# Four graph layers in one kernel: other due dates and buffer reserves for a list scheduler

## The chip, the cores and the metric

The kernel runs on one core of one Trainium2 chip. The metric is the device time of one execution in microseconds. Three executions of the kernel before took 2530.77, 2531.31 and 2533.68 us, so its median is 2531.31 us.

## What is computed

There are 128 graphs of 128 nodes with 256 features each, in fp32. Every layer normalizes its input, applies a ReLU and adds its result to the input:

```python
h = relu(layernorm(x)); x = x + L0(h, adj)   # 3 steps: m = h @ W[i]; a = A^T m; h = GRU(a, h)
h = relu(layernorm(x)); x = x + L1(h, adj)   # sum over relations r: (adj == r) @ h @ W1[r], + bias
h = relu(layernorm(x)); x = x + L2(h, adj)   # attention: softmax(mask(leaky(ei + ej))) @ (h W^T)
h = relu(layernorm(x)); x = x + L3(h, adj)   # the same attention with other weights
```

`GRU` has three gates of two 256x256 products each, so layer 0 holds most of the matrix work. In this text "layer 0" is the recurrent layer and "the attention" or "the later layers" are L1, L2 and L3.

## The kernel before, in words

Four graphs (`G = 4`) make a group of 512 columns; there are 32 groups, numbered 0 to 31. One group passes through loading, layer 0 (three steps, function `step`), the relation layer (`neighbours`, L666, products at L634 and L644) and two attention layers (`attention`, L979, and `attend`, L997), and is then stored (L1087). The gate products of layer 0 are written in a form with seven block products in place of eight; all their matmuls are issued at L825. L767 is the product with the adjacency, also of layer 0.

Nothing in this program runs in the order in which the code is written. `build` (L307) makes a list of operations, each with its engine (some may go to ScalarE or VectorE, as the planner chooses), an assumed duration, its dependences and the buffers that it uses. `Plan.order` (L137) then runs a list scheduler over them in Python, before anything is on the chip, and its result is the fixed order of the instructions on each engine. Four things decide that order:

- **Rank** (L143 to L148). An operation's "way" is the longest chain of assumed durations from it to the end of its own group. Its rank is `group * PERIOD` less its way, less a `rush` that is nonzero for a few operations. The lowest rank goes first. So `group * PERIOD` is a due date of the group, and groups are due 36000 ns apart. (Only differences of rank matter; a group is not finished every 36 us.)
- **Choice** (L225 to L256). On each engine the scheduler looks at the operations whose predecessors are placed. Those that can start within 100 ns of the engine's free time compete by rank; the others come after them by start time. At most `AHEAD = 5` groups are open at a time.
- **Buffers.** A buffer takes a slot of its pool when its first operation is placed and returns it after its last. Pools: 8 PSUM `banks`, 5 `xs`, 7 `adjs`, 29 `big` (128x512 fp32), 11 `wide` (128x1024), 10 `small`, 4 `masks`, 4 `lines`. `SPARE` gives, for the first five pools in that order, how many slots a group later than the oldest open one has to leave free (L236); with `DEEP = 1` the number doesn't grow with the distance.
- **Pieces** (L742, L975). A group is handled as a whole in the later layers, or in pairs of graphs, or singly. With `SINGLE = 2` and `SPLIT = 2`, groups 30 and 31 are handled singly and all others whole. Whole groups turn their attention matrices by a DMA transpose (L362 to L372) and spread a row of terms by two DMAs (L1019, L1021); pairs and singles do both on TensorE (L1012, L1069). The last step of layer 0 in a group that isn't handled whole is turned on TensorE as well (L954).

All four engines' orders, and the transfers issued by SyncE, come from the same plan. The first operations also hold a scan of the whole adjacency (L539 to L548, the last four with a `rush` of 90000), which finds whether all values are 0 or 1. At that point the program branches: `plan.order` is run once for the usual inputs and once, with the operations before the branch as a given `prefix`, for general ones. The inputs here take the usual branch. Some operations (`plan.shared = False`) are planned only after it.

Of the kernel before, what the change touches and what calls it, by code (L numbers as in the profile page):

```python
# [35 lines left out]


OWN = {"PE": 0, "ACT": 125, "DVE": 125, "POOL": 80, "SP": 2500, "ACTQ": 2500}
PERIOD = 36000
AHEAD = 5  # L40
SINGLE = 2
SPLIT = 2
LINE, SPREAD = 0, -1000
TURN = -2000
RUSH = 90000
EARLY = 0
SPARE = (0, 0, 0, 2, 0)
DEEP = 1
LOAD = 2000
BRANCH = 3000  # L50
# [2 lines left out]
def seen(o, h):  # L53
    return o.late + (LAG[o.eng] + HOP[h.eng] if h.engs != (o.eng,) else OWN[o.eng])
# [43 lines left out]
class Plan:  # L98
# [6 lines left out]
    def op(self, eng, ns, fn, r=(), w=(), after=(), port=None, rush=0, late=0):  # L105

        o = Op(*((eng, ns) if isinstance(eng, tuple) else ((eng,), (ns,))), fn, self.group)  # L110
        o.port = eng == "POOL" if port is None else port
        o.rush, o.late = rush, late
        if self.shared:
            o.key = self.keys
            self.keys += 1
        deps = set(after)
        for items, writes in ((r, False), (w, True)):
            for item in items:
                buf, parts = item if isinstance(item, tuple) else (item, None)
                for other, wrote, theirs in buf.uses:  # L120
                    if buf.alone and o.engs + other.engs != ("PE", "PE"):
                        deps.add(other)
                    elif (writes or wrote) and other is not o:
                        if parts is None or theirs is None or parts & theirs:
                            deps.add(other)
                buf.uses.append((o, writes, parts))
                if buf not in o.bufs:
                    o.bufs.append(buf)
                    buf.left += 1
        o.deps = sorted(deps, key=lambda d: d.wait)  # L130
        o.wait = len(self.ops)
        for d in deps:
            d.heirs.append(o)
        self.ops.append(o)
        return o

    def order(self, pools, cut=None, prefix=()):  # L137

        for o in reversed(self.ops):  # L143
            way = max((h.rank + seen(o, h) for h in o.heirs if h.group == o.group), default=0)
            o.rank = way + o.ns
        for o in self.ops:
            o.rank = o.group * PERIOD - o.rank - o.rush
            o.wait = len(o.deps)  # L148
        free = {id(p): [0.0] * len(p) for p in pools}
        spare = {id(p): n for p, n in zip(pools, SPARE)}  # L150
        left = {}
        for o in self.ops:
            left[o.group] = left.get(o.group, 0) + 1
        at = dict.fromkeys(LAG, 0.0)
        port = 0.0
        open_ = {e: [] for e in LAG}
        held = {}
        for o in self.ops:
            if not o.wait:
                held.setdefault(o.group, []).append(o)  # L160
        first = 0

        def admit(o):
            if o.group < first + AHEAD:
                for e in o.engs:
                    open_[e].append(o)
            else:
                held.setdefault(o.group, []).append(o)

        for g in range(AHEAD):  # L170
            for o in held.pop(g, []):
                admit(o)
        done = []

        def place(o, eng, end):
            nonlocal first, port
            for e in o.engs:
                open_[e].remove(o)
            o.eng = eng
            o.end = at[eng] = end  # L180
            if o.port and eng != "ACT":
                port = max(port, end)
            for b in o.bufs:
                b.left -= 1
                if not b.left and id(b.pool) in free:
                    last = max(u.end + u.late + LAG[u.eng] + 60 for u, _, _ in b.uses)
                    free[id(b.pool)][b.slot] = last
            for h in o.heirs:
                h.ready = max(h.ready, o.end + seen(o, h))
                h.wait -= 1  # L190
                if not h.wait:
                    admit(h)
            left[o.group] -= 1
            done.append(o)
            while first in left and not left[first]:
                first += 1
                for x in held.pop(first + AHEAD - 1, []):
                    admit(x)

        def take(b, slot):  # L200
            b.slot = slot
            free[id(b.pool)][slot] = float("inf")

        shared = {o.key: o for o in self.ops if o.key is not None}
        for theirs in prefix:
            o = shared[theirs.key]
            for b, other in zip(o.bufs, theirs.bufs):
                if b.slot is None:
                    take(b, other.slot)
            place(o, theirs.eng, theirs.end)  # L210
            for b, other in zip(o.bufs, theirs.bufs):
                assert b.left or not other.left, "given away too early"
        before = len(done)

        def branch():
            now = max(at[e] for e in ("PE", "ACT", "DVE", "POOL"))
            for e in at:
                at[e] = max(at[e], now + BRANCH)
            return len(done)

        ahead = AHEAD
        if prefix:
            branch()
            ahead = 1
        while len(done) < len(self.ops):  # L225
            best = None
            for eng, cands in open_.items():
                pick = None
                for o in cands:
                    if cut and o.key is None or o.group >= first + ahead:  # L230
                        continue
                    r = o.ready
                    for b in o.bufs:
                        if b.slot is None:

                            kept = spare.get(id(b.pool), 0) * min(o.group - first, DEEP)  # L236
                            r = max(r, sorted(free[id(b.pool)])[kept])
                    if r == float("inf"):
                        continue
                    start = max(at[eng], r, port if o.port and eng != "ACT" else 0)  # L240
                    key = (start if start > at[eng] + 100 else 0, o.rank)
                    if pick is None or key < pick[0]:
                        pick = (key, start, o)
                if pick and (best is None or pick[1] < best[0]):
                    best = (pick[1], pick[2], eng)
            if cut and cut.end and (best is None or best[0] > cut.end + LOAD):
                cut = None
                before = branch()
                continue
            assert best is not None, "no operation can start"  # L250
            start, o, eng = best
            for b in o.bufs:
                if b.slot is None:
                    slots = free[id(b.pool)]
                    take(b, min(range(len(slots)), key=slots.__getitem__))
            place(o, eng, start + o.times[o.engs.index(eng)])  # L256
        return done, before
# [3 lines left out]
def kernel(  # L261
# [45 lines left out]
    def build(general):  # L307
# [227 lines left out]
        for f in range(F):  # L535
# [6 lines left out]
        op("DVE", 120, lambda: nc.vector.tensor_reduce(  # L542
            top.t[:, 0:1], most.t, AX.X, ALU.max), r=[most], w=[top], rush=RUSH)
        op("PE", 109, lambda: nc.tensor.transpose(pm.t[0:1, 0:P], top.t[:, 0:1], ident.t),
           r=[top, ident], w=[pm], rush=RUSH)
        op("DVE", 200, lambda: nc.vector.tensor_reduce(
            top.t[0:1, 1:2], pm.t[0:1, 0:P], AX.X, ALU.max), r=[pm], w=[top], rush=RUSH)
        verdict = op("DVE", 80, lambda: nc.vector.tensor_scalar(  # L548
            found, top.t[0:1, 1:2], 1.0, None, ALU.is_gt), r=[top], rush=RUSH)

# [185 lines left out]
        def group(gi):  # L736
# [4 lines left out]
            xt, ai, aiT = state.pop(gi)  # L741
            pieces = singly if gi >= NG - SINGLE else pairs if gi >= NG - SPLIT else whole  # L742

# [230 lines left out]
            late = [o for o, _, _ in hT.uses[:1]]  # L974
            duos = singly if gi >= NG - SINGLE else pairs  # L975
            (relations if general else neighbours)(gi, xt, ai, aiT, m0, m3, late, pieces, duos)
# [175 lines left out]
```

## Time and profile before

| what | value |
|---|---|
| median of three executions | 2531.31 us |
| the profiled execution: its own time | 2530.32 us |
| the profiled execution: span from first to last instruction | 2528.5 us |
| TensorE busy, share of the span | 2481.2 us, 98% |
| VectorE busy | 2280.3 us, 90% |
| ScalarE busy | 1815.1 us, 72% |
| GpSimd busy | 490.6 us, 19% |
| mean granted TensorE clock | 0.993 |
| last matmul of layer 0 (group 31, L825) starts | 2471.36 us |
| last residual add of layer 0 (L962) starts | 2480.5 us |
| last output transfer issued (L1087) | 2524.0 us |

Matmuls are pipelined: the profile's duration of one matmul (383 ns for 256 columns) is its way through the array, and the next one starts earlier. TensorE is therefore judged by starts: the profile's chain of waits has the same piece of 42 matmuls of L825 begin at 430.06 us and again at 506.03 us, so one group takes 75.97 us in the middle of the run, and 42 matmuls in 9.15 us are 218 ns each. A matmul of 128 columns takes half of that: 16 of L767 that start at 2280.82 us are followed by the next matmul at 2282.61 us, 112 ns each.

### The profile page before, as it was taken

The page shows a single profiled execution, that of the slowest core. Times are in us where ns is not written, and L with a number is a line of the kernel's source. Part 1 is how long each engine was busy: PE and PEld are TensorE (multiplying, and loading weights), DVE is VectorE, ACT ScalarE, POOL GpSimd, SP SyncE. Part 2 cuts the span into 40 slices and gives each one's busy share as a digit, 9 for nine tenths or more (in the row PEclk, how much of TensorE's full clock was granted, in tenths as well). Part 3 has the DMA queues.
Part 4 walks back from the last instruction along what each step waited for, and adds up shares of the span by engine and source line. Part 5 has one row for each costly group of instructions (what it writes and reads, how often), then busy time and mean ns, then how long its engine had stood idle before and what let it go on. Part 6 is the DMA issues. An engine that isn't in the chain of part 4 may idle for free.

```text
span 2528.5 us, 39056 instructions
## 1 busy us (share of the span) xinstructions
PE 2481.2 (98%) x12809; PEld 2192.0 (87%) x12809; DVE 2280.3 (90%) x6543; ACT 1815.1 (72%) x3544; POOL 490.6 (19%) x413
## 2 busy tenths in 40 slices
PE   8999999999999999999999999999999999999996
PEld 7888888888888888888888888888888888888874
DVE  7988889999999999999999989999999999999886
ACT  6667677776677776677776677776677776777653
POOL 1111211122211122111122111122211121222121
PEclk9999999999999999999999999999999999999997
DMA  7511233323233323233323233322333333332200
GB/s 203 141 34 38 54 69 67 74 43 63 60 72 68 71 43 66 60 71 68 65 49 65 62 72 67 63 51 61 65 71 68 58 57 60 67 72 51 47 22 19
DMA packets 424294, 162.82 MB, mean 64 GB/s; under 512 B 343056, under 2 KB 412304, under 8 KB 424080
## 3 DMA queue, kind: packets, MB, share of 16 engines
q1 hardware_dynamic: 422992, 159.18, 30.0%
q8 instruction: 102, 1.67, 0.3%
q10 hardware_dynamic: 1088, 1.05, 0.1%
q14 instruction: 112, 0.92, 0.1%
HBM read 61.48 MB, written 16.90 MB: 31 GB/s over the span
## 4 chain that ended last, share of the span: by engine, by line
PE 95%; DVE 3%; issue 1%; ACT 1%; DMA 0%; POOL 0%; ACTq 0%; DVEq 0%; POOLq 0%
PE bank L825 68%; PE bank L644 13%; PE bank L767 7%; PE bank L634 7%; PE bank L474 1%; DVE small L565 0%; DVE junk L987 0%; DVE big L938 0%; DVE xs L1079 0%; DVE wide L940 0%; DMA big<-in_wihT_dram 0%; DMA big<-big 0%; ACT big L362 0%; PE bank L505 0%; DVE big L913 0%
## 5 line engine op out<-in xcount | busy, mean ns | idle before, releaser
L825 PE MATMUL bank<-big,rz_h 128*128 128x256 f32 x1536 | 463.3, 383 | 1.6 <-ACT big L339 1.0
L339 ACT COPY big<-bank 128x256 f32<-128x256 f32 (+2 forms) x518 | 244.2, 479 | 305.3 <-PE bank L825 246.6
L825 PE MATMUL bank<-big,rz_a 128*128 128x256 f32 x1536 | 456.8, 379 | 0.0
L925 POOL TENSOR_TENSOR big<-wide,big 128x512 f32<-128x512 f32 x192 | 246.4, 1291 | 1031.0 <-ACT big L923 913.6
L842 ACT ACTIVATE big<-big,b_rz 128x256 f32<-128x256 f32 x576 | 269.9, 501 | 173.6 <-DVE big L848 171.7
L362 ACT COPY big<-big 128x1024 uint16<-128x1024 uint16 x270 | 351.0, 1304 | 7.0 <-DMA big<-big 6.2
L591 POOL TENSOR_TENSOR small<-small,nhalf 128x4 f32<-128x4 f32 (+1 forms) x146 | 161.5, 1107 | 978.2 <-DVE small L589 960.1
L825 PE MATMUL bank<-wide,rz_h 128*128 128x256 f32 x1152 | 344.4, 381 | 0.7 <-DVE big L848 0.6
L825 PE MATMUL bank<-wide,rz_a 128*128 128x256 f32 x1152 | 342.6, 379 | 0.0
L825 PEld LDWEIGHTS bank<-big,rz_h 128*128 128x128 f32 x1536 | 281.9, 190 | 54.7 <-DVE big L339 10.4
L825 PEld LDWEIGHTS bank<-big,rz_a 128*128 128x128 f32 x1536 | 291.8, 190 | 39.7
L913 DVE TENSOR_TENSOR big<-bank,big 128x256 f32<-128x256 f32 x672 | 277.2, 417 | 11.9 <-PE bank L825 8.9
L825 PEld LDWEIGHTS bank<-wide,rz_a 128*128 128x128 f32 x1152 | 218.8, 190 | 29.8
L848 DVE TENSOR_TENSOR big<-bank,big 128x512 f32<-128x512 f32 x288 | 197.2, 685 | 48.9 <-PE bank L825 43.8
L825 PEld LDWEIGHTS bank<-wide,rz_h 128*128 128x128 f32 x1152 | 215.8, 190 | 29.0 <-DVE big L848 0.8
L644 PE MATMUL bank<-wa,big 128*128 128x256 f32 x1024 | 235.3, 382 | 0.3 <-ACT big L339 0.3
L339 DVE COPY big<-bank 128x512 f32<-128x512 f32 (+2 forms) x282 | 171.3, 609 | 59.3 <-PE bank L825 35.1
L612 ACT ACTIVATE big<-xs,small 128x256 f32<-128x256 f32 x384 | 200.7, 590 | 33.4 <-DVE small L595 17.6
L825 PE MATMUL bank<-big,n_h 128*128 128x256 f32 x768 | 223.4, 380 | 0.8 <-DVE big L339 0.5
L644 PEld LDWEIGHTS bank<-wa,big 128*128 128x128 f32 x1024 | 195.3, 192 | 27.6 <-ACT big L339 1.1
L825 PE MATMUL bank<-big,n_a 128*128 128x256 f32 x768 | 213.9, 381 | 2.8 <-DVE big L913 2.6
L634 PEld LDWEIGHTS bank<-big,big 128*128 128x128 f32 x1536 | 195.7, 195 | 16.0 <-ACT big L612 8.2
(93 smaller groups left out, 4760.2 us busy)
## 6 DMA issues: line engine op xcount, KB each, us to landing
xs<-in_x_dram SPq DMA_DIRECT2D x64, 256.0 KB, 4.3
big<-line SPq DMA_DIRECT2D x60, 256.0 KB, 3.9
out_dram<-xs SPq DMA_DIRECT2D x30, 512.0 KB, 3.2
adjs<-in_adj_dram SPq DMA_DIRECT2D x32, 256.0 KB, 3.4
adjs<-in_adjT_dram SPq DMA_DIRECT2D x32, 256.0 KB, 3.8
big<-in_adj_dram SPq DMA_DIRECT2D x32, 256.0 KB, 3.1
big<-big SPq DMA_TRANSPOSE x312, 3.1
out_dram<-xs SPq DMA_DIRECT2D x8, 128.0 KB, 2.3
```

The lines of the kernel that those rows point to most:

```text
L339: (nc.scalar.copy if eng == "ACT" else nc.vector.tensor_copy)(dst(), src())
L362: (nc.scalar.copy if eng == "ACT" else nc.vector.tensor_copy)(dst(), src())
L591: op("POOL", 1130, lambda: nc.gpsimd.tensor_tensor(columns(RS), columns(RS), nhalf.t[:, gs.start : gs.stop], ALU.pow), r=[nhalf], w=[own(" ...
L612: nc.scalar.activation(place(g), xt.t[:, g, :].rearrange("p (k m) -> p k m", k=KC), AF.Relu, bias=s.t[:, MR + g : MR + g + 1], scale=s.t[: ...
L634: nc.tensor.matmul(ps.t[:, (len(gs) * k + j) * P : (len(gs) * k + j + 1) * P], hs[g // 2].t[:, (g % 2) * D + k * P : (g % 2) * D + (k + 1) ...
L644: nc.tensor.matmul(ps.t[:, j * D : (j + 1) * D], c.t[:, (len(gs) * k + j) * P : (len(gs) * k + j + 1) * P], w.t[:, k, :], start=(k == 0), ...
L767: nc.tensor.matmul(pg.t[:, g * P : (g + 1) * P], of()[:, g * P : (g + 1) * P], m0.t[:, g, :], start=True, stop=True,)
L825: nc.tensor.matmul(ps.t[:, m * W : (m + 1) * W], a.t[(slice(None), *row, j, slice(m * P, (m + 1) * P))], b[j](), start=(start and m == x = ...
L842: op("ACT", act(W, 1) + 40, lambda m=m, c=c: nc.scalar.activation(t[c].t[:, g2 * W : (g2 + 1) * W], src.t[:, m * W : (m + 1) * W], AF.Tanh ...
L848: op("DVE", dve(T), lambda: nc.vector.tensor_tensor(c.t, ps.t, c.t, ALU.add), r=[ps], w=[c])
L913: op("DVE", dve(W), lambda: nc.vector.tensor_tensor(part(), ps.t[:, :W], part(), ALU.add), r=[ps], w=[(vs[c], {g2})])
L925: op("POOL", 1230, lambda qq=qq, nn=nn, c=c: nc.gpsimd.tensor_tensor(qq.t, hT.t[:, c, :], nn.t, ALU.subtract), r=[(hT, {(c, 0), (c, 1)}), ...
```

## The change

Constants of the scheduler, a second distance of due dates, and one rule of the scheduler that only the general branch can need are changed:

- groups are due 40000 ns apart, but the last two groups only 10000 ns (`CLOSE`) after their predecessors. Groups 28, 29, 30 and 31 were due at 1008, 1044, 1080 and 1116 (in thousands of ns) and are due at 1120, 1160, 1170 and 1180;
- only group 31 is handled singly; group 30 is handled in pairs;
- the rush of the scan's last four operations is 60000;
- later groups leave free one PSUM bank, three `big` and one `wide` buffer (before: two `big`);
- in a plan with a prefix, `ahead` starts at 1 and grows when nothing can start. For a plan without one it stays 5, as before.

No operation is added for groups 0 to 29 and 31; their instructions are reordered. Group 30's later layers are issued in two pieces instead of four.

```diff
-PERIOD = 36000
+PERIOD = 40000
+CLOSE, CLOSING = 10000, 2
 AHEAD = 5
-SINGLE = 2
+SINGLE = 1
 SPLIT = 2
 LINE, SPREAD = 0, -1000
 TURN = -2000
-RUSH = 90000
+RUSH = 60000
 EARLY = 0
-SPARE = (0, 0, 0, 2, 0)
+SPARE = (1, 0, 0, 3, 1)
...
+        last = max(o.group for o in self.ops)
         for o in self.ops:
-            o.rank = o.group * PERIOD - o.rank - o.rush
+            late = max(0, o.group - last + CLOSING)
+            o.rank = (o.group - late) * PERIOD + late * CLOSE - o.rank - o.rush
             o.wait = len(o.deps)
...
+            if best is None and ahead < AHEAD:
+                ahead += 1
+                continue
             assert best is not None, "no operation can start"
+            ahead = 1 if prefix else AHEAD
             start, o, eng = best
```

## The prediction

> **What bounds the kernel now.** I read the page's engine totals first, then a table of busy time by stretches, then the waits of TensorE in the last 200 us, then TensorE's timeline around the last matmul of layer 0.
>
> ```profile
> span 2528.5 us, 39056 instructions
> PE 2481.2 (98%) x12809; PEld 2192.0 (87%) x12809; DVE 2280.3 (90%) x6543; ACT 1815.1 (72%) x3544; POOL 490.6 (19%) x413
> PEclk9999999999999999999999999999999999999997
> ```
>
> TensorE (PE) is busy for 98% of the span, VectorE (DVE) for 90%. The granted clock falls in the last slice only. In the next table the columns are the stretch, its length, the busy time of PE, PEld, DVE, ACT and POOL with instruction counts, the clock, and the DMA share and rate.
>
> ```profile
> 0.00:160.00 160.00, 148.90 (x720) 127.00 (x721) 138.62 (x333) 102.37 (x187) 26.09 (x27) 1.00 0.54 143
> 160.00:2300.00 2140.00, 2138.81 (x11137) 1900.72 (x11137) 1957.27 (x5538) 1581.79 (x3063) 415.65 (x335) 1.00 0.30 62
> 2300.00:2370.00 70.00, 69.43 (x368) 61.35 (x367) 64.40 (x191) 50.73 (x109) 16.25 (x12) 1.00 0.22 50
> 2370.00:2440.00 70.00, 60.63 (x301) 50.62 (x301) 58.97 (x188) 42.84 (x81) 18.10 (x19) 0.99 0.18 38
> 2440.00:2472.00 32.00, 31.91 (x172) 27.57 (x171) 25.87 (x118) 17.59 (x55) 2.20 (x4) 0.97 0.05 18
> 2472.00:2528.50 56.50, 31.56 (x121) 24.78 (x120) 35.15 (x179) 19.82 (x55) 12.26 (x18) 0.71 0.04 11
> ```
>
> From 160 to 2300 us TensorE is idle for 1.2 us in all: nothing can be won there, only lost. The head has 11.1 us of idle time, 6.5 of them waiting for the first weights, which the change doesn't touch. The end has 9.4 us of idle in 2370 to 2440 and then a last stretch of 56.5 us with 121 matmuls, where the middle would have started 295 (11137 in 2140 us). So the end is where the change can win.
>
> ```profile
> PE bank L1012 <- DVE small L987: 10.0, 7, 2.5
> PE bank L634 <- ACT big L612: 6.9, 2, 5.5
> PE bank L954 <- DVE wide L940: 5.1, 1, 5.1
> PE bank L644 <- ACT big L339: 1.8, 4, 0.6
> ```
>
> These are the waits (total, times, longest). They are links of a serial chain: norm, terms (L987), row, softmax, product, with no other group's work to lie beside it.
>
> ```profile
> 2471.36 0.69 PE L825 MATMUL bank<-wide,n_a 128*128 128x256 f32 x2
> 2477.18 1.97 PE L954 MATMUL bank<-ident,wide 128*128 128x128 f32 x8 [5.13 <-DVE wide L940]
> 2484.68 2.08 PE L634 MATMUL bank<-big,big 128*128 128x128 f32 x8 [5.53 <-ACT big L612]
> ```
>
> The last gate product starts at 2471.4. All that follows is group 31: its three later layers, alone, 56.5 us from 2472.
>
> **What the Trainium skill says.** "Perfetto Trace Analysis", Identifying Performance Opportunities, Optimization Strategy, says that a kernel whose most contended engine changes over time may gain by interleaving its regimes. That is this end: layer 0 is TensorE's regime, the later layers VectorE's. Its part on identifying the most-contended engine warns that matmul busy time doesn't show the distance from the roofline; the trace agrees: the last stretch reads 31.6 us busy for 121 matmuls, some 17.6 us at the steady spacing. "TensorE: Matmul & The Clock Gate", HAM oscillation, says that an idle gap over about 3.4 us brings the half clock back; here the gaps of 5.13 and 5.53 us stand beside a clock of 0.71.
>
> **The change, part by part.**
>
> *Due dates.* What counts is the difference of ranks (due less remaining way). Ways are the scheduler's own, so I estimate them from the trace. Group 31, single, takes from its last residual add (2480.5) to its last store issue (2524.0) 43 us. Group 29, whole, takes from its residual (2319.6) to its store (2414.8) 95 us under load; unloaded I take 60, between both. Group 30 in pairs: 47, a little over the single one. Before, the end of group 31's layer 0 had rank 1116 - 43 = 1073; operations of group 30 (due 1080) lie behind it only with a way under 7. The trace agrees: group 30's last product runs 2466.3 to 2469.9, just ahead of the last L825. After, that rank is 1180 - 43 = 1137. Group 30 (due 1170) is behind with ways under 33: two of three later layers. Group 29 (due 1160) is behind with ways under 23: about one layer. So three group-layers of later work move behind the last L825.
>
> TensorE: a group-layer is 16 matmuls at L634 of 0.11 us and 16 at L644 of 0.217 = 5.2 us; three, with group 30's transposes (16 of 0.11, of which about half move), 16.5 us. The last L825 comes at 2472.0 - 16.5 = 2455.5. With three groups' layer 0 side by side, the 9.4 us of idle in 2370 to 2440 should shrink; I take half, 4.7, so **2450.8**. Bounds: none (2455.5) or all (2446.1).
>
> VectorE then: group 31's own 35.2 us (table) plus three moved layers. The rows for the later layers give per group: L565 4.5 (12 of its 16), L987 7.4, L1079 3.8, L1041 2.6, L1038 1.4, L675 1.4, small statistics 3.4, reciprocals 0.5, its share of evictions 1.5: 26.5 us, 8.8 per layer. 35.2 + 26.5 = 61.7 us. The middle keeps VectorE at 70.04 of 75.97 us, 92%: 61.7 / 0.92 = **67 us**. Group 31's chain alone is 56.5, so VectorE becomes what sets the end. Bounds: 61.7 (VectorE without a gap) to 76 (81% dense, as in 2440 to 2472, where group 30's later layers already alternate with layer 0: 25.87 of 32 us). ScalarE has less (19.8 us plus three layers of some 5). End: 2450.8 + 67 = 2517.8, a gain of 10.7 us. Bounds: 2446.1 + 61.7 = 2507.8 (gain 20.7) and 2455.5 + 76 = 2531.5 (loss 3).
>
> *Queues that are passed.* Moved later layers of group 29 bring their DMAs with them: row spreads (3.9 us to landing) and transposes (3.1) stand later in SyncE's queue, near no load, since the last loads are issued at about 2250. GpSimd's powers (L591, 1.1 us) are three more in the last stretch, where GpSimd is busy 12 of 56 us. Both lie beside VectorE's work; without that cover a late whole group would add one spread and one transpose, 7 us, inside the upper bound.
>
> *Clock.* More matmuls after 2450 should shorten the gaps of over 5 us. The last stretch shows about 14 us more busy time than its matmuls need, part of it slow clock. It is on group 31's chain, not on VectorE's sum: counted at nothing; if the chain binds, worth up to 7 us, inside the lower bound.
>
> *Pairs for group 30.* Fewer, wider small operations. In singles a layer's six small statistics take four instructions each of about 0.15 us in place of one of 0.15 to 0.37; some of these overlap. Two pieces fewer save at most 3 layers x 6 x 2 x 0.07 = 2.5 us of VectorE; the longer chain per piece costs a similar size. Taken as zero.
>
> *Period 40 and SPARE.* In the middle TensorE has 75.97 us of work per group, VectorE 70.0: any order that keeps a ready product in front of TensorE costs nothing. The reserve of one bank of 8, one wide of 11 and three big of 29 narrows what later groups may start. The trace doesn't show how near the pools are to empty. Bounds: 0, and the second rival's price. I take 0. There is no gain to exclude or include: 1.2 us idle.
>
> *Rush 60000, and the branch.* The scan's last four operations total 0.8 us; later or earlier verdict moves work that is planned only after it. The head's idle time other than the first weights is 4.6 us: between -3 and +3, taken as 0. The growing `ahead` concerns the general branch, which isn't run.
>
> *Sum.* -10.7 in 2530.32 of the profiled execution is 2519.6; the median of runs stands 1.0 above that execution, 2520.6. **Predicted: 2521 us**, 0.4% faster.
>
> **Rivals.** *First, the end is merely exchanged*: VectorE's sum with poor packing, 76 us, or buffers that keep group 31 from being brought forward at all (it needs an `xs` slot from group 26, stored only at 2246). Both end within 5 us of now: 2527 to 2534, taken as 2531. For it: VectorE has slack in layer 0 now that later layers fill, and taking them out wastes it. Against: 57 us with one group alone is a lot to fill.
>
> *Second, slower: the reserve starves TensorE in the middle.* A bubble repeated for every group. The skill's page on trace analysis, in the part on the most-contended engine, says that consistent bubbles can mean too little buffer space; no bubble repeats in this trace. Its price is that of the waits in 140 to 152 us, 0.34 and 1.36 us: I take 0.9 us x 29 groups = 26 us, so 2521 + 26 = 2547. It decides from 10.7 / 29 = 0.37 us per group on, when the whole gain of the end is eaten. For it: three pools are narrowed and pieces in flight are fewer with period 40. Against: TensorE's 0.84 ns per column in the plan (PE_COL) is a little less than the 0.85 measured (217 ns for 256), so the other engines have slack that the plan doesn't count.
>
> *Third, better than forecast*: all idle in 2370 to 2440 filled and VectorE dense: 2510.
>
> **How the numbers follow.** Forecast (2513 to 2526) 0.50; third rival 0.10; first 0.18; second 0.22. A measurement of this kernel can tell some 0.2%, 5 us, from no change. Faster: 0.50 + 0.10 + 0.02 of the first = 0.62; same 0.16 of the first and 0.01 of a weak second = 0.17; slower 0.21. The range must leave out no more than 0.2: from 2508 (the low bound of the end) to 2538, which takes in the first rival and the weaker half of the second. The likeliest case's own range is 2513 to 2526.
>
> **What would show it.** Right: the last L825 before 2460 us; group 30's and 29's L644 after it; VectorE over 85% busy from there to the end; the middle's idle of TensorE still under 3 us. Wrong: idle that recurs every 76 us; the last L825 still near 2470; a stretch after it as long as 76 us or more, with VectorE below 80%; or a head that is longer by over 3 us.

## The result, and the profile after

The changed kernel takes 2536.49 us (median of 20 executions, 2535.06 to 2538.15); the kernel before, run beside it, 2533.23 (20 executions, 2528.10 to 2536.02). The ratio is 1.0015, 95% interval 1.0008 to 1.0022: slower by 0.15%, where 0.4% faster was forecast. The profiled execution took 2536.27 us with a span of 2534.3 us, 5.8 us more than the span of before. Lines of the code have moved by 7: L825 is now L832 (gate products), L925 is L932 (GpSimd's difference), L987 is L994 (attention terms), L938 and L940 are L945 and L947.

The page of the changed kernel, totals of the engines:

```profile
span 2534.3 us, 39147 instructions
PE 2480.1 (98%) x12809; PEld 2184.6 (86%) x12809; DVE 2267.5 (89%) x6423; ACT 1867.4 (74%) x3606; POOL 479.9 (19%) x405
```

Little can be read from these; the busy shares are within two points of those of before. The same table of stretches as for before (stretch, length, busy time and count of PE, PEld, DVE, ACT, POOL, clock, DMA) shows where the time went:

```profile
0.00:160.00 160.00, 150.03 (x738) 130.53 (x739) 137.19 (x327) 103.83 (x196) 25.13 (x26) 1.00 0.58 143
160.00:2300.00 2140.00, 2120.83 (x11027) 1875.17 (x11026) 1942.16 (x5446) 1621.52 (x3095) 412.33 (x335) 1.00 0.30 61
2300.00:2370.00 70.00, 70.00 (x360) 62.03 (x359) 58.74 (x157) 48.02 (x96) 11.16 (x10) 1.00 0.23 42
2370.00:2440.00 70.00, 69.40 (x368) 61.67 (x367) 57.47 (x155) 46.36 (x95) 11.58 (x9) 1.00 0.23 46
2440.00:2472.00 32.00, 23.85 (x106) 18.46 (x105) 28.23 (x109) 19.92 (x48) 8.51 (x8) 0.88 0.11 17
2472.00:2534.30 62.30, 45.94 (x218) 36.75 (x216) 43.76 (x234) 27.77 (x80) 11.20 (x18) 0.80 0.08 27
```

Matmuls are counted, since there is the same number in both programs; one is worth 0.192 us on average (2140 us for 11137 in the middle of before). The head has 18 more: 3.5 us won. The middle has 110 fewer: **21.1 us lost**. From 2300 us on, before took 228.5 us for 957 matmuls and after 234.3 for 1047: 90 more at 0.192 is 17.3, so the end is **11.5 us better**. The sum, -3.5 + 21.1 - 11.5, is +6.1, and the span grew by 5.8; the three parts add up by the way they are made, so this tests none of them. Run e2 below does: it differs from the changed kernel in the due distance and the reserves alone and is 18.6 us faster than before, where the changed kernel is 3.3 slower. The 21.9 us between them agree with the 21.1. So the end did what the change is for, and the middle, for which the forecast had taken 0, cost more than that.

TensorE's waits between 160 and 2300 us (who waited for whom, total, times, longest), where before there was 1.2 us of idle time in all:

```profile
PE bank L832 <- DVE big L902: 11.3, 26, 0.5
PE bank L832 <- ACT big L346: 5.9, 23, 0.5
```

26 and 23 waits in some 28 groups: one of each in nearly every group. The chain of waits gives the period (start, length, what):

```profile
484.68 6.91 PE bank L832 x32
...
561.42 6.91 PE bank L832 x32
```

76.74 us from one group to the next, where before it was 75.97. This is the second rival's picture: a gap that comes back with every group, 0.77 us of it.

What holds L902 up is seen on GpSimd and VectorE in the same 10 us of one group. (The tiles named `bank` lie in PSUM, all others here in SBUF.) GpSimd's timeline (start, length, engine, line, operation, idle time before it):

```profile
1051.37 1.27 POOL L932 TENSOR_TENSOR big<-wide,big 128x512 f32<-128x512 f32 x1 [1.55 <-ACT big L930]
1052.60 1.46 POOL L632 TENSOR_TENSOR xs<-xs,b_s 128x512 f32<-128x512 f32 x1
1056.11 1.27 POOL L932 TENSOR_TENSOR big<-wide,big 128x512 f32<-128x512 f32 x1 [2.05 <-ACT big L930]
1057.34 1.71 POOL L632 TENSOR_TENSOR xs<-xs,b_s 128x512 f32<-128x512 f32 x1
```

VectorE's:

```profile
1051.07 0.41 DVE L994 CUSTOM_DVE_ANT_0 junk<-big,ub 128x256 f32<-128x256 f32 x1
...
1051.41 1.52 DVE L994 CUSTOM_DVE_ANT_0 junk<-big,ub 128x256 f32<-128x256 f32 x1
...
1052.86 0.68 DVE L855 TENSOR_TENSOR big<-bank,big 128x512 f32<-128x512 f32 x1
...
1055.20 0.67 DVE L945 SCALAR_TENSOR_TENSOR big<-big,big 128x512 f32<-128x512 f32 x1
...
1056.40 1.53 DVE L947 SCALAR_TENSOR_TENSOR wide<-big,big 128x512 f32<-128x512 f32 x1
1057.85 1.75 DVE L945 SCALAR_TENSOR_TENSOR big<-big,big 128x512 f32<-128x512 f32 x1
```

The same L994 takes 0.41 us, and 1.52 when L932 runs beside it: L932 ends at 1052.64, this L994 at 1052.93. The same L945 takes 0.67 and then 1.75, beside L632, which ends at 1059.05, 0.55 us before it. So the held instruction stands still until GpSimd's has ended and then still takes most of its own time. VectorE is busy without a pause from 1041 to 1060 us here, so what it is held up by comes out at the end, at L902; that last step is argued here and tested by the experiments. In the order of before, at the like place of a group, the same lines of GpSimd meet a VectorE that waits for TensorE or reads PSUM:

```profile
1044.78 1.27 POOL L925 TENSOR_TENSOR big<-wide,big 128x512 f32<-128x512 f32 x1 [0.63 <-ACT big L923]
1046.01 2.50 POOL L625 TENSOR_TENSOR xs<-xs,b_s 128x512 f32<-128x512 f32 x2
1045.43 0.69 DVE L848 TENSOR_TENSOR big<-bank,big 128x512 f32<-128x512 f32 x1 [0.35 <-PE bank L825]
1047.16 0.69 DVE L848 TENSOR_TENSOR big<-bank,big 128x512 f32<-128x512 f32 x1 [1.04 <-PE bank L825]
```

The Trainium skill, "GPSIMD Engine Reference", Specifications, says that GpSimd shares its SBUF interfaces with VectorE, and that VectorE's instructions contend with it when they have two SBUF inputs or run in a 2-port performance mode. The trace agrees: L855, with one operand in PSUM, keeps its 0.68 us in the midst of L632, and L920, also with one in PSUM, has a mean of 417 ns in both kernels, while L994, with both in SBUF, went from 417 to 484. Two forms with a single SBUF input were held as well, L369's copy and L754 (see the last section); whether they run in that mode, no view shows.

The scheduler knows of this contention, by a fifth rule beside the four that are listed ahead: an operation marked `port` (L111 of the kernel before; all of GpSimd's but its powers, and many of VectorE's) is planned to start only when the last such operation on the other engine has ended (L181, L240). But a plan leaves only an order on each engine. On the chip L932 starts as soon as its inputs are there (above, when ScalarE's L930 is done), whether or not the VectorE instructions that were planned ahead of it have run. How often the two change places is counted below.

### The profile page after: what moved, and what is told of

Its sections match the earlier page's. It is cut to its first block, busy times and chain, and to the rows that moved or that the text cites. A ratio compares the mean times of both kernels' runs of the same rounds, so it can differ in the third digit from the quotient of the medians.

```text
span 2534.3 us, 39147 instructions
## 1 busy us (share of the span) xinstructions
PE 2480.1 (98%) x12809; PEld 2184.6 (86%) x12809; DVE 2267.5 (89%) x6423; ACT 1867.4 (74%) x3606; POOL 479.9 (19%) x405
## 3 DMA queue, kind: packets, MB, share of 16 engines
q1 hardware_dynamic: 422960, 159.18, 29.8%
## 4 chain that ended last, share of the span: by engine, by line
PE 76%; DVE 15%; ACT 5%; issue 3%; DMA 1%; POOL 0%; ACTq 0%; DVEq 0%; SPq 0%
PE bank L832 55%; PE bank L651 9%; PE bank L774 6%; PE bank L641 5%; DVE big L945 3%; DVE junk L994 2%; ACT big L369 2%; ACT big L1041 1%; DVE big L920 1%; DVE big L346 1%; DVE small L572 1%; DVE big L902 1%; DVE wide L947 1%; DMA big<-big 1%; DVE big L855 1%
## 5 line engine op out<-in xcount | busy, mean ns | idle before, releaser
L932 POOL TENSOR_TENSOR big<-wide,big 128x512 f32<-128x512 f32 x192 | 246.9, 1293 | 1172.4 <-ACT big L930 1117.2
L832 PE MATMUL bank<-big,rz_h 128*128 128x256 f32 x1536 | 457.9, 380 | 1.2 <-DVE big L346 1.0
L832 PE MATMUL bank<-big,rz_a 128*128 128x256 f32 x1536 | 457.0, 379 | 0.0
L346 ACT COPY big<-bank 128x512 f32<-128x512 f32 (+2 forms) x508 | 243.6, 491 | 200.7 <-PE bank L832 139.2
L369 ACT COPY big<-big 128x1024 uint16<-128x1024 uint16 x287 | 367.9, 1283 | 16.7 <-DMA big<-big 15.4
L832 PE MATMUL bank<-wide,rz_a 128*128 128x256 f32 x1152 | 342.8, 379 | 0.1
L832 PE MATMUL bank<-wide,rz_h 128*128 128x256 f32 x1152 | 342.8, 379 | 0.0
L832 PEld LDWEIGHTS bank<-big,rz_a 128*128 128x128 f32 x1536 | 291.7, 190 | 40.0 <-DVE big L805 0.2
L920 DVE TENSOR_TENSOR big<-bank,big 128x256 f32<-128x256 f32 x672 | 273.0, 417 | 55.1 <-PE bank L832 54.0
L832 PEld LDWEIGHTS bank<-big,rz_h 128*128 128x128 f32 x1536 | 282.6, 190 | 37.1 <-DVE big L346 1.8
L598 POOL TENSOR_TENSOR small<-small,nhalf 128x4 f32<-128x4 f32 (+2 forms) x140 | 136.1, 973 | 855.7 <-DVE small L596 825.4
L369 ACT COPY big<-wide 128x1024 uint16<-128x1024 uint16 x189 | 197.7, 1047 | 92.3 <-DVE small L602 67.4
L832 PEld LDWEIGHTS bank<-wide,rz_a 128*128 128x128 f32 x1152 | 218.7, 190 | 30.4 <-ACT wide L346 0.8
L651 PE MATMUL bank<-wa,big 128*128 128x256 f32 x1024 | 236.2, 383 | 0.7 <-ACT big L346 0.7
L832 PEld LDWEIGHTS bank<-wide,rz_h 128*128 128x128 f32 x1152 | 213.9, 190 | 26.4
L832 PE MATMUL bank<-big,n_h 128*128 128x256 f32 x768 | 229.4, 383 | 6.5 <-ACT big L346 5.9
L855 DVE TENSOR_TENSOR big<-bank,big 128x512 f32<-128x512 f32 x288 | 196.6, 684 | 39.8 <-PE bank L832 35.7
L994 DVE CUSTOM_DVE_ANT_0 junk<-big,ub 128x256 f32<-128x256 f32 x512 | 228.7, 484 | 1.0 <-ACT big L619 1.0
L832 PE MATMUL bank<-big,n_a 128*128 128x256 f32 x768 | 220.2, 382 | 3.5 <-DVE big L920 3.4
L346 DVE COPY big<-bank 128x512 f32<-128x512 f32 (+2 forms) x282 | 161.0, 586 | 67.1 <-PE bank L832 49.4
```

The source lines that it names most:

```text
L346: (nc.scalar.copy if eng == "ACT" else nc.vector.tensor_copy)(dst(), src())
L369: (nc.scalar.copy if eng == "ACT" else nc.vector.tensor_copy)(dst(), src())
L598: op("POOL", 1130, lambda: nc.gpsimd.tensor_tensor(columns(RS), columns(RS), nhalf.t[:, gs.start : gs.stop], ALU.pow), r=[nhalf], w=[own(" ...
L651: nc.tensor.matmul(ps.t[:, j * D : (j + 1) * D], c.t[:, (len(gs) * k + j) * P : (len(gs) * k + j + 1) * P], w.t[:, k, :], start=(k == 0), ...
L832: nc.tensor.matmul(ps.t[:, m * W : (m + 1) * W], a.t[(slice(None), *row, j, slice(m * P, (m + 1) * P))], b[j](), start=(start and m == x = ...
L855: op("DVE", dve(T), lambda: nc.vector.tensor_tensor(c.t, ps.t, c.t, ALU.add), r=[ps], w=[c])
```

## Experiments

All times are medians, beside runs of the kernel before on the same chip (2532.3 to 2533.0). Two numbers go with each: the matmuls started between 500 and 2000 us (7814 before, 7727 in the changed kernel; 10 fewer are some 0.1 us per group), and the time per group that VectorE was **held**. That is worked out from VectorE's groups of instructions by shape in that window: mean less the mean of the same shape in the run e10, where nothing is held, times the count, over 19.7 groups. Before: 30 us, L579 (416 against 155 ns, 80 times) and L940 (763 against 684, 118 times), 1.5 us per group. After: 88 us, 4.5 per group. Of the instructions in that window that took 60 ns or more over their usual time, all stood beside one of two lines of GpSimd: L932 (58 us) and L632, the bias of the relation layer (31 us).

**e1, the reserves of before** (`SPARE = (0, 0, 0, 2, 0)` in the changed kernel).

> The changed kernel with the buffer reserves of before; due dates 40 us apart, the last two 10 us. Theory R (the reserves make the middle longer): a group takes 75.97 us in the middle again, idle time of TensorE from 160 to 2300 us falls from 19.2 to under 3 us, and the time to 2536 - 22 = 2514 us. Theory P (the due distance of 40 us makes the middle longer): a group still takes some 76.7 us, idle time stays at 15 to 20 us, and the time stays near 2536 us.

2518.34 us (ratio 0.9942, 0.9925 to 0.9958); idle time in the middle 10.6 us, 7769 matmuls, held 3.7. Half and half: the reserves cost, and the due distance costs.

**e2, the end only** (the changed kernel with `PERIOD = 36000` and the reserves of before).

> The changed kernel with the due distance of 36 us and the reserves of before, so that only the end (close due dates, one group single) and the rush differ from the kernel before. Both theories: the middle is that of before, 75.97 us per group and under 3 us of idle time, and the end keeps its gain of about 12 us: 2533 - 12 = 2521 us. If the end's gain is only time that the changed head or middle moved elsewhere, it is 2531 to 2535 us.

2513.86 us (0.9923, 0.9907 to 0.994), 7 us better than expected. The middle is that of before to the matmul (7814, held 1.6), and the end's gain stands alone.

**e3, the new reserves with the due dates of before** (the changed kernel with `PERIOD = 36000`, `CLOSE = 36000`, `SINGLE = 2`).

> The due dates and pieces of before (36 us everywhere, two groups single), with the new reserves and the rush of 60000. Theory R: the middle is 76.7 us per group or more, 20 us of idle time in it, 2533 + 22 = 2555 us. Theory P: the middle is that of before, and the time is 2533 us within 5.

2557.29 us (1.0096, 1.0079 to 1.0113); 7744 matmuls, idle 12.5 us in the middle, held 3.7.

**e4, the due distance alone** (the kernel before with `PERIOD = 40000`).

> The kernel before with due dates 40 us apart and nothing else. Theory P: 76.7 us per group, 15 to 20 us of idle time in the middle, 2533 + 22 = 2555 us. Theory R: 75.97 us per group, 2533 us within 10, since the last group may end a few us later behind its predecessors.

2557.94 us (1.0099, 1.0082 to 1.0116); 7776 matmuls, held 3.7. Its idle time in the middle is only 11.5 us; the rest is the end, where the last L825 now starts at 2500.86. So neither theory was whole: reserves and due distance each lengthen the middle, and in each case the held time has gone from 1.5 to 3.7.

**e5 and e6, which reserve** (the changed kernel with `SPARE = (0, 0, 0, 3, 1)` and `(1, 0, 0, 2, 0)`).

> The changed kernel without the reserve of a PSUM bank; the reserves of three big and one wide buffer stay. Theory B (of the three reserves the bank's is the one that costs): as with all reserves of before, some 10 us of idle time of TensorE between 160 and 2300 us instead of 19, and 2518 us. If the big or wide reserve costs: 19 us idle, 2536 us.

> The changed kernel with the reserve of one PSUM bank alone (two big as before, no wide). Theory B: 19 us of idle time in the middle, 2536 us. If big or wide cost: some 10 us, 2518 us.

e5: 2532.06 us (1.0001, 0.9992 to 1.001), 7730 matmuls, held 4.6. e6: 2530.03 us (0.9989, 0.9981 to 0.9998), 7769 matmuls, held 3.8. The bank's reserve isn't the one: without it the middle is as bad as in the changed kernel. The reserve in `big` and `wide` takes the held time from 3.7 to 4.6; that of the bank costs its 12 us against e1 outside the steady part (43 fewer matmuls by 2300 us, 20 of them in the first 160).

**e7, more room in the plan** (`LAG` of ScalarE and VectorE 160 and 135 ns in place of 110 and 85).

> The changed kernel with 50 ns more assumed between the end of an operation on ScalarE or VectorE and the start of its successor on another engine, so that the scheduler leaves more room. Theory T (the new order places products right behind their evictions and any delay on VectorE opens a gap): the idle time of the middle falls from 19 to under 8 us and the time to 2522 or less. Theory D (the delay itself, on VectorE, is the cause and isn't moved by 50 ns): idle time of 12 us or more, 2530 us or more.

2556.15 us (1.0094, 1.0077 to 1.0111); 7646 matmuls, held 5.9. The theory that the products only stand too close behind their evictions got no support: with more room assumed, TensorE lost more. But the other lags also made another order, in which VectorE was held more, so the run doesn't test the room by itself.

**e8, one single group without close due dates** (`CLOSE = 36000` in e2).

> The kernel before with one group single in place of two and the rush of 60000, due dates and reserves as before: what the close due dates alone are worth is the difference to the run with the end only (2513.9). If the close due dates bring the gain of the end: 2533 us within 3, and the last L825 (here L832) near 2470 us. If handling group 30 in pairs brings it: 2515 to 2520 us.

2532.38 us (0.9998, 0.9989 to 1.0007). Handling group 30 in pairs, together with the rush of 60000, is worth nothing; the close due dates are worth 2532.38 - 2513.86 = 18.5 us.

**e9, the differences issued by VectorE, in the order of the changed kernel.**

```diff
-                    op("POOL", 1230, lambda qq=qq, nn=nn, c=c: nc.gpsimd.tensor_tensor(
+                    op("POOL", 1230, lambda qq=qq, nn=nn, c=c: nc.vector.tensor_tensor(
```

> The changed kernel in its own order, with GpSimd's 192 differences (L932, 1.29 us each) issued by VectorE at the same places of the order. Theory D (VectorE's instructions stand still while GpSimd runs that difference, and the new order lets more of them collide): the long VectorE instructions disappear (L994 from 484 to some 417 ns, L945 from 859 to some 690), TensorE's idle time from 160 to 2300 us falls from 19 to under 5 us, time 2536 - 15 = 2521 us or less, although VectorE gets 6 x 0.6 = 3.6 us more to do per group. Theory F (VectorE has too much to do in the new order, whoever holds it up): idle time 15 us or more, 2533 us or more.

2511.07 us (0.9919, 0.9902 to 0.9936), 25.4 less than the changed kernel whose order it has; 7841 matmuls, held 1.1. Its stretch of the middle, and its L994 and L947 in 500 to 2000 us (count, busy, mean ns):

```profile
160.00:2300.00 2140.00, 2138.05 (x11174) 1903.22 (x11174) 1977.48 (x5679) 1645.13 (x3144) 201.97 (x168) 1.00 0.30 62
```

```profile
L994 DVE CUSTOM_DVE_ANT_0 junk<-big,ub 128x256 f32<-128x256 f32 x320 | 121.5, 416 | 0.0
L947 DVE SCALAR_TENSOR_TENSOR wide<-big,big 128x512 f32<-128x512 f32 x118 | 80.0, 678 | 0.0
```

In the changed kernel these two were:

```profile
L994 DVE CUSTOM_DVE_ANT_0 junk<-big,ub 128x256 f32<-128x256 f32 x320 | 143.8, 486 | 0.0
L947 DVE SCALAR_TENSOR_TENSOR wide<-big,big 128x512 f32<-128x512 f32 x116 | 99.5, 857 | 0.0
```

The middle now has 147 more matmuls than the changed kernel and 37 more than before, with VectorE given 3.6 us more work per group. This also excludes two rivals. It isn't the sum of VectorE's work that lengthens the group: between 500 and 2000 us it is busy for 1360 us in the changed kernel, less than before (1382), and for 1384 in e9. Nor is it that the new plan gave more of the shared work to ScalarE (1108 us busy before, 1147 after): in e9 it has 1163.

**e10, the same in e2.**

> The run with the end only (2513.9), with the same 192 differences issued by VectorE. Theory D: the middle has no idle time to win (1.1 us); the stalls there (1.6 us per group) go, so the middle stays at 75.97 us per group; the end may win the 1 to 3 us of its stalls: 2511 to 2515 us. Theory F: 3.6 us more per group on a VectorE that is at 70 of 76 us opens gaps: 2518 us or more.

2524.20 us (0.9969, 0.9957 to 0.998), a miss: 10 us worse than e2, held 0.0, 7781 matmuls. This order had been made for a VectorE without the differences, and few of them had been in its way; the likely reading is that the added work costs there and the freed time is small. So the held time isn't the only thing that lengthens the middle: work on VectorE that the plan doesn't know of does it too. No idle time shows for it, 1.4 us in 500 to 2000; see the last section.

**e11, the differences planned on VectorE, all constants of the change kept** (`op("DVE", dve(T), ...nc.vector...)`, marked `port`).

> The changed kernel with the differences on VectorE and planned there (dve(T), with the port), all its other constants kept: due distance 40, its reserves. Theory D: with no long GpSimd instruction in the way, due distance and reserves cost nothing in the middle: idle time under 5 us, 2513 to 2522 us. If due distance or reserves cost by themselves: 10 us of idle time or more, 2525 us or more.

2502.01 us (0.9879, 0.9863 to 0.9896), better than either theory's range. 7858 matmuls, held 0.1; the last L832 starts at 2430.62. With the collisions gone no cost of the due distance of 40 and the reserves is left to see in the middle: e15 below, with the old ones, has 7830.

**e12, the last groups 5 us apart in e2** (`CLOSE = 5000`).

> The run with the end only, with the last two groups 5 us apart instead of 10. The more layer 0 goes ahead the more of the later layers is left for the stretch behind it, where VectorE is 74% busy in 73.3 us: I expect the last layer-0 product 2 to 5 us earlier, the stretch as much longer, and 2514 us within 3. If the chain of the last group sets the end: 2509 to 2511 us.

2509.00 us (0.991, 0.9893 to 0.9926). The last layer-0 product is 4 us earlier (2435.37) and the stretch behind it isn't longer (72.1 us against 73.3). The time is that of the second theory, but VectorE's work in the stretch didn't grow either (54.7 us against 54.4), so its sum was not put to the test.

**e13, the collisions added to the order of before**: one more GpSimd instruction behind every second difference.

```diff
+                    def differ(qq=qq, nn=nn, c=c):
+                        nc.gpsimd.tensor_tensor(qq.t, hT.t[:, c, :], nn.t, ALU.subtract)
+                        if c:
+                            nc.gpsimd.tensor_tensor(spin.t, spin.t, spin.t, ALU.subtract)
```

> The kernel before in its own order, with one more GpSimd instruction of the same form and size (on a tile that nothing else uses, so no result depends on it) after every second of the 192 differences: three more per group, which the scheduler doesn't know of. Theory D: VectorE stands still some 2 to 3 us more per group (from 1.5 to about 4 us, as in the changed kernel), the middle loses 70 to 100 matmuls of its 7814 between 500 and 2000 us, and the time is 2548 to 2560 us. If the colliding instructions are harmless and only the order matters: 2533 us within 3. A part of any loss can come from a later difference or norm on GpSimd, 1.3 us each.

2562.81 us (1.0119, 1.0102 to 1.0136), 29.8 us more than before; held 3.6 per group, 7742 matmuls. The order is that of before and no product depends on the added instruction. The time is just over the expected range. The reservation made there, that a later difference or norm is held behind the added instruction on GpSimd, doesn't apply between 500 and 2000 us: each of the 59 added instructions there is followed by a norm's power (L593) that starts 1.4 us or more after it has ended and was waiting for VectorE, as here:

```profile
1066.11 1.04 POOL L930 TENSOR_TENSOR spin<-spin 128x512 f32<-128x512 f32 x1
1069.80 1.02 POOL L593 TENSOR_TENSOR small<-small,nhalf 128x4 f32<-128x4 f32 x1 [2.64 <-DVE small L591]
```

So nothing on GpSimd was delayed by them there, and the holding is what is left to explain the 72 matmuls that this window lost.

**e14 and e15, the best version, and what the change is worth in it**: e11 with `CLOSE = 5000`, and the kernel before with the differences planned on VectorE.

> The changed kernel with the differences planned on VectorE (2502.0) and the last two groups 5 us apart instead of 10. If the chain of the last group sets the end, as the 5 us that the same step won on the run with the end only say: 2497 to 2500 us. If VectorE's work sets it, now that it has the differences too: 2501 us or more.

> The kernel before with the differences planned on VectorE and all constants of before. It tells what the change is worth when no GpSimd product is in VectorE's way: the middle in 75.6 to 76.0 us per group, the end that of before, so 2518 to 2530 us, 16 to 28 us above the same edit on the changed kernel (2502.0). If the change's constants are worth nothing once the collisions are gone: 2502 us within 4.

e14: **2494.98 us** (0.9854, 0.9837 to 0.987), the fastest of all and better than either range. Its last L832 starts 11.4 us earlier than in e11 (2419.24), and the stretch behind it is 3.4 us longer (73.0 us against 69.6) with 2.9 us more of VectorE's work (55.3 against 52.4). e15: 2526.13 us (0.9972, 0.9963 to 0.998), 7830 matmuls. The change is worth 2526.13 - 2502.01 = 24.1 us on a kernel without GpSimd's differences, and minus 3.3 on the kernel with them.

## Why the prediction was wrong

**The end: mechanism right, sizes off.** Three group-layers were to move behind the last product of layer 0. They did: in e2, whose middle is that of before, 234 matmuls lie behind it (121 before), and three layers of 32 and 16 transposes make up 112 of the difference. The last product was forecast at 2450.8 and starts at 2439.57. The term that was mis-sized is the time got back, put at 4.7 us, half of the 9.4 us of idle time. Idle time isn't all that was lost there. Counting 216 ns for a matmul of 256 columns and 112 for one of 128 (the medians of the starts between 500 and 2000 us), the 834 matmuls of before from 2300 us to the last of layer 0 need 155.6 of 171.7 us: 16.1 us lost, of which 10.0 show as idle time. In e2, 712 need 135.9 of 139.9 us, so 12.1 us came back. The moved matmuls are worth 17.5 us by the same count (16.5 in the forecast), and the head gave 2.6. (By this count the 121 matmuls of before's last stretch need 18.6 us, not the prediction's 17.6.) The stretch behind it was forecast at 67 us and takes 73.3 to 73.5. VectorE was to set it, with 61.7 us at 92%; it has 54.4 us of work there, so the three moved layers brought it 19.2 us and not 26.5, and it is 74% busy:

```profile
2440.00:2513.30 73.30, 50.68 (x234) 40.74 (x232) 54.44 (x275) 35.23 (x102) 13.85 (x20) 0.79 0.09 27
```

What sets it instead stays open. In e2 the profile's chain of waits runs through TensorE for half of this stretch (25.2% at L651, 18.3 at L641, 5.3 at L1076, 1.8 at L961); in e14 the stretch grew about as VectorE's work did. The two errors have opposite signs, 11.2 us early and 6.3 us long, and leave an end at 2513.3 for the forecast's 2517.8: that this part of the sum came out is in part luck.

**The middle: the step that failed.** "Period 40 and SPARE ... I take 0": measured 0.77 us per group, 21.1 us in all, twice the 10.7 us that the forecast had won at the end. The reason given, that any order which keeps a ready product in front of TensorE costs nothing, holds only where the products are ready; that depends on how long VectorE's instructions last, and I took their durations from rows of the old order, as if they went with the instruction. They go with what runs beside it. The profile of before had a sign of it: L579, a subtraction of 4 columns, with a mean of 372 ns beside others of its kind with some 155, and L940 with 760 beside L938 with 698.

```profile
L579 DVE TENSOR_TENSOR small<-small 128x4 f32<-128x4 f32 x122 | 45.4, 372 | 0.2
L940 DVE SCALAR_TENSOR_TENSOR wide<-big,big 128x512 f32<-128x512 f32 x192 | 145.4, 760 | 0.0
```

**The second rival** had the picture (a gap per group, deciding from 0.37 us on) and nearly the size (0.9 us), but its cause, too few buffers, was only the occasion. Reserves and due distance each choose another order (e1, e3, e4, e5), and in each of them VectorE is held for 3.7 to 4.6 us per group in place of 1.5. e9 takes most of the holding out of the changed order and the loss goes with it; e13 puts it into the old order and a loss comes. With the differences planned elsewhere the same reserves show no cost (e11). e10 limits this: with nothing held, but work added that the plan doesn't know of, the middle lost 33 matmuls.

**"There is no gain to exclude or include: 1.2 us idle"** was wrong too. e11's middle holds 7858 matmuls against 7814, 75.55 us per group against 75.97. Nor is it so that no gap repeats in before: its starts show the same six in every group, each 50 to 150 ns long, some 0.5 us together, of which nearly nothing is recorded as idle time (last section).

**Zero terms**: pairs held (e8, with the rush). The clock of the last stretch rose from 0.71 to 0.79 in e2; what that is worth no run tells. The head gained 3.5 us, just over its bound of 3.

**Why the new order collides more, and what stays open.** The held instructions of the traces can be matched with the same operations in the scheduler's plan. Before, between 500 and 2000 us, 39 are held by 60 ns or more, 30 us in all, and in all 39 the plan too has GpSimd's operation first: the wait had been counted. In the changed kernel 136 are held, 89 us in all, and in 78 of them, 65 us, the plan has VectorE's first, but the chip ran GpSimd's first. e1 has 64 such among 118 (59 of 72 us). So the rise is one of collisions that the plan believed it had avoided. No run made GpSimd wait for its planned turn, so that this is enough to remove the loss is not shown. Open too is how much of e9's gain is the difference's own latency (1.29 us on GpSimd, some 0.6 on VectorE); in e13 that latency is unchanged, so the holding costs without it.

## What to carry to other kernels

A change of scheduling constants is a new order everywhere, so price the stretch that it isn't meant for first, and by counting instructions of the bound engine in a fixed window. Where GpSimd and VectorE both read SBUF, as here, a recorded duration needn't belong to the instruction: compare the mean of a shape with its shortest, and treat the difference as a cost that the next order can multiply (1.5 to 4.5 us per group here). A planner's rule against a collision holds only as far as something on the chip keeps its order. In a schedule that is close to its bound, try taking such a shared resource out before any finer ordering: here moving 192 differences of 1.29 us to the busier engine, and planning them there, turned a change worth +3.3 us into one worth -24.1.

## What the runs showed of the hardware

- A VectorE instruction with both inputs in SBUF stands still until a GpSimd instruction of 128x512 elements that runs beside it ends: 0.41 to 1.52 us for L994, 0.67 to 1.75 for L945. In the changed kernel, between 500 and 2000 us, the 39 L947 that began beside L932 have a mean of 1217 ns, the other 77 of 675.
- Of the forms with one SBUF input, two were held in the changed kernel: L369's copy of 1024 16-bit elements (1402 ns, 743 in e10) and L754 (562, 409 in e10). The statistics L565 were not: 120 of them began beside L925 or L591 in before, none of which took over 420 ns. Nor are those with one operand in PSUM: 39 L855 beside L932 or L632 have a mean of 685 ns, the others 684.
- Not every GpSimd instruction holds: beside the power L598 (4 columns, 1.01 us) 40 L994 of e9 took 418 ns. And GpSimd is slowed as well: L632 has a mean of 1.27 us before and 1.59 in the changed kernel (40 each).
- TensorE's busy share hides short gaps. Between 500 and 2000 us it reads 1499.8 us for before with 7814 matmuls, 1498.6 for e10 with 7781 and 1499.5 for e11 with 7858. These rows are e10's and e11's:

```profile
500.00:2000.00 1500.00, 1498.61 (x7781) 1327.10 (x7780) 1409.47 (x4004) 1099.62 (x2126) 148.41 (x119) 1.00 0.30 63
```

```profile
500.00:2000.00 1500.00, 1499.50 (x7858) 1340.84 (x7858) 1398.58 (x4020) 1119.64 (x2184) 128.92 (x118) 1.00 0.31 64
```

The starts show the gaps. Starts that come more than 20 ns later than the median spacing (216 ns, 112 after a matmul of 128 columns) are 123 in before, 148 in e10 and 47 in e11, and are late by 11.0, 16.9 and 3.3 us in all. The idle time recorded between the same matmuls is 0.2, 1.4 and 0.5 us: a matmul of 256 columns is recorded with 380 ns, so a start can come some 160 ns late without leaving any. The weight loads don't hide the lost time: PEld reads 1327 and 1341 us in these two.
